# Sums over two channel blocks in a state-space layer's output stage, made by GpSimd instead of TensorE

## The chip, the cores and the metric

The kernel runs on one core of one Trainium2 chip. The metric is the device time of one execution in microseconds (us). Engines are named as in the profile: PE is TensorE, PEld its loading of weights, DVE VectorE, ACT ScalarE, POOL GpSimd, SP SyncE, which here issues the DMAs. L491 is line 491 of the kernel before; the changed file has its lines a few numbers further down.

## The reference, cut to what matters

Four layers are run one after the other on an image of 2 x 56 x 56 positions with 128 channels. The change concerns the end of the first layer, a selective scan in two dimensions. Its input is normalized by groups and projected to twice 256 channels, `x` and `z`. The first 256 go through a 3 x 3 convolution and four scans (by rows and by columns, each forwards and backwards), whose sum is `y`. Then:

```
mu  = jnp.mean(y, axis=-1, keepdims=True)
var = jnp.mean((y - mu) ** 2, axis=-1, keepdims=True)
y = (y - mu) / jnp.sqrt(var + EPS) * out_norm_w + out_norm_b
y = y * z
return jnp.einsum('bhwd,cd->bhwc', y, out_proj_w) + out_proj_b
```

Here `z` has already gone through silu, and the mean runs over the 256 channels of a position. The result is added to the layer's input. The second layer is another scan of the same kind with four heads one after the other; the third and fourth hold attention and other mixers.

## The kernel before, in words

Positions number L = 3136 in each of two batches; a chunk is 448 of them, so there are seven chunks a batch. In the scan layers channels lie on the 128 partitions and positions along the free axis. The 256 inner channels are two blocks of 128, `ci` 0 and 1, and `y[0]` and `y[1]` are the two halves of the buffer `pair`, each 128 x 3136 in float32.

The first layer goes: preparation of batch 0 (`before`, chunk by chunk), scans of batch 0 (`scans.run`), then in one loop over chunks the outputs of batch 0 (`after`, L671) and the preparation of batch 1 (`before`, L635), scans of batch 1, then in one loop the outputs of batch 1 and the preparation of the second layer's first head (L830). So `after` runs fourteen times, in two stretches of seven, each beside the preparation of the scans that follow.

The scans carry their own written order (`manual_schedule`). Outside of them a planner places each engine's instructions by its own estimates, so the order on an engine is not the order of the source, and a change of one function can move its neighbours. Each engine then works through its list in order.

One chunk of `after`: SP loads the kept normalized input (`hout`) and the layer's input `xr`; POOL adds a bias to `xr` (L679); PE projects `hout` to the gate, one product for each block (`pz`, L683), and ACT applies silu (L687). Then `gated_tokens`: PE multiplies both blocks of `y` by a matrix whose entries are all 1/256 (`avg`) and accumulates the two, so that `pm` holds the mean of the 256 channels on every partition (L491). DVE subtracts it from each block (`yc`, L495), ACT squares (`sq0`, `sq1`, L497), POOL multiplies `yc` by the gate (L499). For each of four groups of TP = 112 positions PE makes three sums over both blocks (L509): the variance `pv` (the squares against a column of `avg`), `p1` (the gated `yc` against the output weights) and `p2` (the gate against the bias term's weights); the result has positions on partitions. ACT takes the root (L511), DVE the reciprocal (L512), and DVE scales `p1`, adds `xr` and `p2` and writes the result to `X` (L691 to L693).

Beside it in the first stretch is the convolution of batch 1: nine products on PE (L460) or nine steps on DVE (L464, L466), silu on ACT (L467), and a copy into the transposed order on POOL (L468). In the second stretch it is the second layer's normalization (L78 to L86; L83 takes the root on ACT, L86 is on POOL), scaling of copies on POOL (L848, L849), transposes (L852), projection (L855, L867) and convolution. The pieces that begin a scan (`first`, L230) lie in the same stretches.

Of buffers, the pool `one` has a single one for each name: `sq0`, `sq1`, `xr`, `t`. The PSUM pool `pp` of `pm`, `pv`, `p1`, `p2`, `pz` has one each too. Tiles from `sp` (`yc0`, `yc1`, `z0`, `z1`, `rs`, `hout`) have two. ACT must load another table when it goes from silu to the root, the exponential or softplus; these appear as loads of their own.

Of the kernel before, what the change touches and what calls it, by code (L numbers as in the profile page):

```python
# [14 lines left out]
F32 = mybir.dt.float32  # L15
BF16 = mybir.dt.bfloat16
AF = mybir.ActivationFunctionType
ALU = mybir.AluOpType
# [7 lines left out]
TP = 112  # L26
NT = L // TP
CH = 448
# [449 lines left out]
    nc.gpsimd.memset(pad[:, :, PAD - 1 : PAD], 0.0)  # L478


def gated_tokens(k, pools, nch, y, gate, avg, mean, w1, w2, c, nb):

    nc = k.nc
    sp, pp, one = pools
    cs = slice(CH * c, CH * (c + 1))
    pm = pp.tile([128, CH], F32, name="pm")
    for ci in range(nch):  # L490
        nc.tensor.matmul(pm, lhsT=avg, rhs=y[ci][:, cs], start=ci == 0, stop=ci == nch - 1)  # L491
    sq, yz = [], []
    for ci in range(nch):
        yc = sp.tile([128, CH], F32, name=f"yc{ci}")
        nc.vector.tensor_tensor(yc, y[ci][:, cs], pm, ALU.subtract)  # L495
        s = one.tile([128, CH], F32, name=f"sq{ci}")
        nc.scalar.activation(s, yc, AF.Square)  # L497
        sq.append(s)
        nc.gpsimd.tensor_tensor(yc, yc, gate[ci], ALU.mult)  # L499
        yz.append(yc)  # L500
    n = w1[0].shape[-1]
    pv = pp.tile([TP, 4 * nb], F32, name="pv")
    p1 = pp.tile([TP, 4, n], F32, name="p1")
    p2 = pp.tile([TP, 4, n], F32, name="p2")
    for i in range(4):
        ts = slice(TP * i, TP * (i + 1))
        for out, m, rhs in ((pv[:, nb * i : nb * (i + 1)], sq, [mean] * nch), (p1[:, i], yz, w1), (p2[:, i], gate, w2)):
            for ci in range(nch):
                nc.tensor.matmul(out, lhsT=m[ci][:, ts], rhs=rhs[ci], start=ci == 0, stop=ci == nch - 1)  # L509
    rs = sp.tile([TP, 4 * nb], F32, name="rs")  # L510
    nc.scalar.activation(rs, pv, AF.Sqrt, bias=k.eps[:TP])  # L511
    nc.vector.reciprocal(rs, rs)  # L512
    return p1, p2, rs
# [45 lines left out]
def layer0(k, d, big, follow):  # L559


    nc, tc, X = k.nc, k.tc, k.X
    with ExitStack() as ctx:
# [13 lines left out]
        avg = wp.tile([128, 128], F32, name="avg0")  # L577
# [3 lines left out]
        y, row, col = ([t[:, 0:L] for t in big[i : i + 2]] for i in (0, 2, 4))  # L581
# [28 lines left out]
        with ExitStack() as sctx:  # L610
# [47 lines left out]
            def outputs(ip):  # L658

                ow = load(nc, ip, d["L0_out_w"], "out_w")  # L660
                outs = []
                for n in ("onw", "onb"):
                    t = ip.tile([128, 2, C], F32, name="outonw") if n == "onw" else ow
                    for ci in range(2):
                        nc.vector.tensor_scalar(t[:, ci], ow[:, ci], W[n][:, ci : ci + 1], None, ALU.mult)
                    outs.append([t[:, ci] for ci in range(2)])
                bias = ip.tile([TP, C], F32, name="out_b0")
                nc.sync.dma_start(bias, d["L0_out_b"][0].partition_broadcast(TP))
                return outs, bias

            def after(b, pools, c, outs, bias):  # L671


                sp, pp, one = pools
                h = sp.tile([128, CH], F32, name="hout")
                nc.sync.dma_start(h, kept[b, :, CH * c : CH * (c + 1)])
                xr = one.tile([TP, 4, C], F32, name="xr")
                nc.sync.dma_start(xr, d["x"][b, CH * c : CH * (c + 1)].rearrange("(j p) c -> p j c", p=TP))
                nc.gpsimd.tensor_tensor(xr, xr, bias.unsqueeze(1).to_broadcast([TP, 4, C]), ALU.add)  # L679
                gate = []  # L680
                for ci in range(2):
                    ps = pp.tile([128, CH], F32, name="pz")
                    nc.tensor.matmul(  # L683
                        ps, lhsT=W["in_w"][:, 256 + 128 * ci : 384 + 128 * ci], rhs=h, start=True, stop=True
                    )
                    z = sp.tile([128, CH], F32, name=f"z{ci}")
                    nc.scalar.activation(z, ps, AF.Silu, bias=W["in_b"][:, 2 + ci : 3 + ci])  # L687
                    gate.append(z)
                p1, p2, rs = gated_tokens(k, pools, 2, y, gate, avg, avg[:, 0:1], outs[0], outs[1], c, 1)
                t = one.tile([TP, 4, C], F32, name="t")  # L690
                nc.vector.tensor_tensor(t, p1, rs.unsqueeze(2).to_broadcast([TP, 4, C]), ALU.mult)  # L691
                nc.vector.tensor_tensor(xr, xr, p2, ALU.add)
                nc.vector.tensor_tensor(  # L693
                    X[:, 4 * c : 4 * (c + 1), b, :].rearrange("p j (c g) -> p j g c", g=4),
                    t.rearrange("p j (g c) -> p j g c", g=4), xr.rearrange("p j (g c) -> p j g c", g=4), ALU.add,
                )

            for b in range(B):
                with ExitStack() as bctx:
                    sp = bctx.enter_context(k.pool(f"mid{b}", 2))  # L700
                    pp = bctx.enter_context(k.pool(f"pmid{b}", psum=True))
                    cp = bctx.enter_context(k.pool(f"pcon{b}", 2, psum=True))
                    ip = bctx.enter_context(k.pool(f"pads{b}"))
                    if b > 0:
                        outs = outputs(ip)
# [17 lines left out]
                    for c in range(NCH + 1):  # L723
                        if b == 0 and c == 2:
                            norm(1, (ap, tp), groups)
                        if b > 0 and c < NCH:
                            after(b - 1, (sp, pp, ip), c, *outs)
                        before(b, (sp, cp), c, pads, diag)
                        if c == 2:
                            scans.first(cp)  # L730
                scans.run()
        with ExitStack() as bctx:
            sp = bctx.enter_context(k.pool("midl", 2))
            pp = bctx.enter_context(k.pool("pmidl", psum=True))
            ip = bctx.enter_context(k.pool("onel"))
            outs = outputs(ip)
            chunk = follow(bctx)
            for c in range(NCH + 1):
                if c < NCH:
                    after(B - 1, (sp, pp, ip), c, *outs)  # L740
                chunk(c)
# [1302 lines left out]
```

## Time and profile before

| | |
|---|---|
| median of 3 runs | 9105.64 us (9102.32 to 9109.07) |
| the profiled execution, its own time | 9098.37 us |
| its span | 9096.6 us |
| PE busy | 7993.2 us (88%) |
| DVE busy | 7088.0 us (78%) |
| POOL busy | 6350.1 us (70%) |
| ACT busy | 3854.8 us (42%) |
| mean granted PE clock | 0.951 |

The span is the time from the first to the last recorded instruction of one execution, which was taken by the hardware profiler; that execution's own time is a little more. The busy shares are averages over stages with different limits: what an edit is worth is read in its own stage. A matrix product in float32 leaves two records on PE here, so that the 28 products into `pm` are counted as 56.

### The profile page before, as it was taken

The page shows a single profiled execution, that of the slowest core. Times are in us where ns is not written, and L with a number is a line of the kernel's source. Part 1 is how long each engine was busy: PE and PEld are TensorE (multiplying, and loading weights), DVE is VectorE, ACT ScalarE, POOL GpSimd, SP SyncE. Part 2 cuts the span into 40 slices and gives each one's busy share as a digit, 9 for nine tenths or more (in the row PEclk, how much of TensorE's full clock was granted, in tenths as well). Part 3 has the DMA queues.
Part 4 walks back from the last instruction along what each step waited for, and adds up shares of the span by engine and source line. Part 5 has one row for each costly group of instructions (what it writes and reads, how often), then busy time and mean ns, then how long its engine had stood idle before and what let it go on. Part 6 is the DMA issues. An engine that isn't in the chain of part 4 may idle for free. (4 is left out here: it accounts for less than half of the span.)

```text
span 9096.6 us, 93496 instructions
## 1 busy us (share of the span) xinstructions
PE 7993.2 (88%) x28687; PEld 4765.5 (52%) x28687; DVE 7088.0 (78%) x7568; ACT 3854.8 (42%) x6644; POOL 6350.1 (70%) x4066
## 2 busy tenths in 40 slices
PE   8888888888887888888888888699999999999998
PEld 4444445444444444444444444355688888874555
DVE  8999998999997997998999899511467667665442
ACT  4555545555555555554554555433211111114331
POOL 6999996999996997998899799566311111115551
PEclk9999999999999998998999899799999999999999
DMA  5666664666664995996898699100233333320004
GB/s 159 221 221 220 222 212 127 221 221 220 222 220 110 230 226 134 227 228 157 203 227 204 157 227 224 39 3 3 85 96 105 104 94 110 93 63 8 14 1 135
DMA packets 780368, 1362.92 MB, mean 150 GB/s; under 512 B 133101, under 2 KB 405486, under 8 KB 779834
## 3 DMA queue, kind: packets, MB, share of 16 engines
q1 hardware_dynamic: 779866, 1356.95, 53.1%
q8 instruction: 227, 3.72, 0.2%
q14 instruction: 275, 2.25, 0.1%
HBM read 1317.03 MB, written 39.60 MB: 149 GB/s over the span
## 5 line engine op out<-in xcount | busy, mean ns | idle before, releaser
L430 POOL TENSOR_TENSOR p<-h,c 128x784 f32<-128x784 f32 x2048 | 3761.2, 1864 | 115.0 <-DVE h L358 33.1
L358 DVE TENSOR_TENSOR_SCAN h<-a,state,h 128x784 f32<-128x784 f32 x1536 | 2791.8, 1840 | 51.6 <-ACT a L339 28.7
L378 PE MATMUL acc<-p,center 128*128 128x392 f32 x4096 | 1499.0, 499 | 22.7 <-POOL p L430 20.8
L378 PE MATMUL acc<-p,ident 128*128 128x392 f32 x4096 | 1491.9, 498 | 6.7 <-POOL p L430 6.7
L417 DVE TENSOR_TENSOR h<-du,b 128x784 f32<-128x784 f32 x1408 | 1336.7, 949 | 75.6 <-PE b L364 70.4
L339 ACT ACTIVATE a<-delta,L0A 128x784 f32<-128x784 f32 x1024 | 939.3, 918 | 973.4 <-DVE h L358 971.5
L339 ACT ACTIVATE a<-delta,L1A 128x784 f32<-128x784 f32 x1024 | 939.2, 917 | 908.3 <-DVE h L358 905.3
L364 PE MATMUL b<-three,sel 96*128 96x512 bf16 (+1 forms) x2816 | 728.6, 341 | 563.9 <-DVE h L417 460.1
L433 POOL TENSOR_TENSOR h<-du,b 128x784 f32<-128x784 f32 x640 | 1190.3, 1860 | 4.1 <-PE pcv L460 4.1
L378 PEld LDWEIGHTS acc<-p,center 128*128 128x128 f32 x4096 | 740.9, 192 | 536.8 <-POOL p L430 60.2
L378 PEld LDWEIGHTS acc<-p,ident 128*128 128x128 f32 x4096 | 743.9, 192 | 512.8 <-POOL p L430 26.5
L1089 POOL TENSOR_TENSOR total<-total,e 128x448 f32<-128x448 f32 (+1 forms) x644 | 735.6, 1142 | 326.0 <-ACT e L1078 286.0
L358 DVE TENSOR_TENSOR_SCAN h<-a,h 128x784 f32<-128x784 f32 x512 | 901.7, 1780 | 36.7 <-ACT a L339 21.1
L364 PEld LDWEIGHTS <-sel 96*128 96x128 bf16 x2816 | 281.5, 100 | 1230.9 <-issue 1048.6
L1572 DVE TENSOR_TENSOR u<-u,cv 128x512 f32<-128x512 f32 x1024 | 623.7, 681 | 326.6 <-PE cv L1559 325.4
L1603 POOL TENSOR_TENSOR u<-u,S 128x1024 f32<-128x1024 f32 x64 | 150.0, 2365 | 1041.0 <-DVE S L1572 1041.0
L1078 ACT ACTIVATE e<-sc 128x448 f32<-128x448 f32 (+1 forms) x700 | 377.2, 543 | 723.0 <-PE sc L1076 596.3
L1574 ACT COPY u<-cv 128x512 f32<-128x512 f32 x256 | 149.5, 587 | 829.3 <-PE cv L1559 775.7
L1673 PE MATMUL pj<-u,Wm 128*128 128x196 f32 (+8 forms) x1536 | 354.7, 384 | 5.7 <-DVE A L1679 5.7
L1076 PE MATMUL sc<-big 128*128 128x448 f32 (+1 forms) x700 | 323.4, 547 | 15.4 <-ACT e L1078 12.3
L1070 PE MATMUL av<-e,big 128*128 128x448 f32 (+1 forms) x700 | 320.9, 545 | 1.2 <-DVE e L1083 1.0
L1653 POOL TENSOR_TENSOR both<-mpm 128x512 f32<-128x512 f32 x32 | 40.6, 1269 | 392.3 <-DVE Wm L1709 272.8
(452 smaller groups left out, 11251.1 us busy)
## 6 DMA issues: line engine op xcount, KB each, us to landing
c<-rows SPq DMA_DIRECT2D x1024, 392.0 KB, 4.0
c<-rows SPq DMA_DIRECT2D x2048, 196.0 KB, 4.8
b<-rows SPq DMA_DIRECT2D x320, 392.0 KB, 4.5
b<-rows SPq DMA_DIRECT2D x640, 196.0 KB, 4.6
H<-raw SPq DMA_DIRECT2D x32, 1568.0 KB, 7.6
wC<-win SPq DMA_DIRECT2D x64, 576.0 KB, 6.4
w<-in_L_weight_dram SPq DMA_DIRECT2D x52, 512.0 KB, 6.3
wA<-win SPq DMA_DIRECT2D x64, 384.0 KB, 5.6
```

Of the source, the lines that this page charges most:

```text
L339: self.k.nc.scalar.activation(x["a"], g["delta"][ci], AF.Exp, scale=self.w["A"](g["kd"], ci, x["n"]))
L358: self.k.nc.vector.tensor_tensor_scan(h, a, h, start, ALU.mult, ALU.add)
L364: self.k.nc.tensor.matmul(ps[:, c0:c1], lhsT=self.w["selB"](x["n"]), rhs=x["g"]["three"][:, c0:c1], start=True, stop=True)
L378: nc.tensor.matmul(job["acc"][:, i, 0:392], lhsT=self.w["sum"], rhs=x["p"][:, 392 * i : 392 * (i + 1)], start=False, stop=n == NS - 1,)
L417: nc.vector.tensor_tensor(one["h"], one["g"]["du"][one["ci"]], one["b"], ALU.mult)
L430: nc.gpsimd.tensor_tensor(now["p"], now["h"], now["c"], ALU.mult)
L433: nc.gpsimd.tensor_tensor(three["h"], three["g"]["du"][three["ci"]], three["b"], ALU.mult)
L1076: nc.tensor.matmul(ps[:n], lhsT=keys[b][:, KT * j : KT * j + n], rhs=q, start=True, stop=True)
L1078: nc.scalar.activation(e[:n], ps[:n], AF.Exp, scale=scale)
L1089: nc.gpsimd.tensor_tensor(total[:n], total[:n], e[:n], ALU.add)
L1572: nc.vector.tensor_tensor(place(o), place(o), ps, ALU.add)
L1673: nc.tensor.matmul(ps[:, lo - c0 : hi - c0], lhsT=Ws[f][:, eo, r, :], rhs=u[:, b, f, lo - a0 : hi - a0], start=f == 0, stop=f == 1,)
```

## The change

In `gated_tokens` POOL adds the two blocks of `y` first, into a tile `both`, and PE multiplies that one tile by `avg`. After both squares are made, POOL adds the second to the first, and PE makes each of the four pieces of `pv` from that sum in one product. `both` has the name `sq1` and so uses the buffer of the second square. The products that remain are also written in another order: all of `p2`, all of `p1`, then `pv`. Three parameters that had only one value in use go.

```diff
-def gated_tokens(k, pools, nch, y, gate, avg, mean, w1, w2, c, nb):
+def gated_tokens(k, pools, y, gate, avg, w1, w2, c):
...
+    both = one.tile([128, CH], F32, name="sq1")
+    nc.gpsimd.tensor_tensor(both, y[0][:, cs], y[1][:, cs], ALU.add)
     pm = pp.tile([128, CH], F32, name="pm")
-    for ci in range(nch):
-        nc.tensor.matmul(pm, lhsT=avg, rhs=y[ci][:, cs], start=ci == 0, stop=ci == nch - 1)
+    nc.tensor.matmul(pm, lhsT=avg, rhs=both, start=True, stop=True)
...
         nc.gpsimd.tensor_tensor(yc, yc, gate[ci], ALU.mult)
         yz.append(yc)
+    nc.gpsimd.tensor_tensor(sq[0], sq[0], sq[1], ALU.add)
     n = w1[0].shape[-1]
-    pv = pp.tile([TP, 4 * nb], F32, name="pv")
+    pv = pp.tile([TP, 4], F32, name="pv")
     p1 = pp.tile([TP, 4, n], F32, name="p1")
     p2 = pp.tile([TP, 4, n], F32, name="p2")
-    for i in range(4):
-        ts = slice(TP * i, TP * (i + 1))
-        for out, m, rhs in ((pv[:, nb * i : nb * (i + 1)], sq, [mean] * nch), (p1[:, i], yz, w1), (p2[:, i], gate, w2)):
-            for ci in range(nch):
-                nc.tensor.matmul(out, lhsT=m[ci][:, ts], rhs=rhs[ci], start=ci == 0, stop=ci == nch - 1)
+    tiles = [slice(TP * i, TP * (i + 1)) for i in range(4)]
+    for p, m, w in ((p2, gate, w2), (p1, yz, w1)):
+        for i, ts in enumerate(tiles):
+            for ci in range(2):
+                nc.tensor.matmul(p[:, i], lhsT=m[ci][:, ts], rhs=w[ci], start=ci == 0, stop=ci == 1)
+    for i, ts in enumerate(tiles):
+        nc.tensor.matmul(pv[:, i : i + 1], lhsT=sq[0][:, ts], rhs=avg[:, 0:1], start=True, stop=True)
...
-                p1, p2, rs = gated_tokens(k, pools, 2, y, gate, avg, avg[:, 0:1], outs[0], outs[1], c, 1)
+                p1, p2, rs = gated_tokens(k, pools, y, gate, avg, outs[0], outs[1], c)
```

More of the change, by code (lines that the diff above doesn't have):

```diff
@@ L500, in gated_tokens @@
         yz.append(yc)
+    nc.gpsimd.tensor_tensor(sq[0], sq[0], sq[1], ALU.add)
     n = w1[0].shape[-1]
-    pv = pp.tile([TP, 4 * nb], F32, name="pv")
+    pv = pp.tile([TP, 4], F32, name="pv")
     p1 = pp.tile([TP, 4, n], F32, name="p1")
     p2 = pp.tile([TP, 4, n], F32, name="p2")
-    for i in range(4):
-        ts = slice(TP * i, TP * (i + 1))
-        for out, m, rhs in ((pv[:, nb * i : nb * (i + 1)], sq, [mean] * nch), (p1[:, i], yz, w1), (p2[:, i], gate, w2)):
-            for ci in range(nch):
-                nc.tensor.matmul(out, lhsT=m[ci][:, ts], rhs=rhs[ci], start=ci == 0, stop=ci == nch - 1)
-    rs = sp.tile([TP, 4 * nb], F32, name="rs")
+    tiles = [slice(TP * i, TP * (i + 1)) for i in range(4)]
+    for p, m, w in ((p2, gate, w2), (p1, yz, w1)):
+        for i, ts in enumerate(tiles):
+            for ci in range(2):
+                nc.tensor.matmul(p[:, i], lhsT=m[ci][:, ts], rhs=w[ci], start=ci == 0, stop=ci == 1)
+    for i, ts in enumerate(tiles):
+        nc.tensor.matmul(pv[:, i : i + 1], lhsT=sq[0][:, ts], rhs=avg[:, 0:1], start=True, stop=True)
+    rs = sp.tile([TP, 4], F32, name="rs")
     nc.scalar.activation(rs, pv, AF.Sqrt, bias=k.eps[:TP])
```

## The prediction

> **What bounds the kernel now.** I read the page for the whole, then, for the two stretches in which the changed function runs, busy times, groups of instructions and the time line. The chain that ended last covers only the program's final instructions and says nothing here.
>
> The products into the tile `pm` (count, least/median/most ns, first to last start):
>
> ```profile
> L491 PE MATMUL pm<-pair,avg x56: 539/539/643, 1364.3 to 2826.9; 128*128 128x448 f32 x56
> ```
>
> The busy times of the two stretches and of the second one's tail (start:end, length, busy us of PE, PEld, DVE, ACT, POOL, then the granted PE clock, DMA share, GB/s):
>
> ```profile
> 1362.70:1490.90 128.20, 116.00 (x534) 75.55 (x534) 92.85 (x140) 68.26 (x97) 53.62 (x47) 0.97 0.18 50
> 2750.00:2885.00 135.00, 106.10 (x514) 67.80 (x513) 85.17 (x159) 82.74 (x119) 61.96 (x66) 0.90 0.14 34
> 2845.00:2885.00 40.00, 25.04 (x74) 13.22 (x73) 21.11 (x36) 23.98 (x30) 13.66 (x11) 0.71 0.06 15
> ```
>
> Only 263 us of 9097 are touched: seven chunks between batch 0's scans and batch 1's (first stretch), seven between batch 1's scans and the second layer's (second). The scans on either side have a written order and take none of it. In the first stretch PE is busy for 116 of 128 us: it sets the pace, with short waits. In the second it is busy for 106 of 135, but only 25 of the last 40, where a chain through all engines decides.
>
> The time line of PE through a chunk, then DVE's and POOL's at the same place (start, length, operation, number of records; what it waited for in brackets):
>
> ```profile
> 1397.02 1.64 PE L509 MATMUL pv<-avg,sq 128*112 128x1 f32 x16
> 1398.53 1.00 PE L646 MATMUL pcv<-hin,L0in_w 128*128 128x448 f32 x2
> ...
> 1402.34 0.47 PE L509 MATMUL p<-outonw,yc 128*112 128x128 f32 x2 [2.07 <-POOL yc L499]
> ...
> 1403.62 1.67 PE L491 MATMUL pm<-pair,avg 128*128 128x448 f32 x4
> 1405.13 0.60 PE L509 MATMUL p<-out_w,z 128*112 128x128 f32 x4
> ```
>
> ```profile
> 1391.91 6.74 POOL L468 COPY big<-big 128x448 f32<-128x448 f32 x1 [4.96 <-ACT big L467]
> ...
> 1412.80 6.58 DVE L466 SCALAR_TENSOR_TENSOR cv<-pad,L0taps,cv 128x448 f32<-128x448 f32 x5
> ```
>
> A product leaves two records. Eight `pv` products hold PE from 1397.02 to 1398.53, so 0.19 us each; two `pm` products from 1403.62 to 1405.13, so 0.75 us each. PE waits in between for `yc`, which POOL makes. And POOL and DVE block one another: a copy that takes 0.99 us alone took 6.74 while DVE ran its convolution, and five steps of that convolution took 6.58 instead of 5 x 0.68 = 3.4 while POOL was at work.
>
> **What the Trainium skill says.** "SBUF — State Buffer", Who interferes with whom: a DVE instruction with two SBUF inputs and a GpSimd instruction that reads SBUF exclude each other for the whole instruction, whichever begins first. The convolution step (`pad`, `cv`) has two such inputs, `yc`'s subtraction has one and a PSUM bank; the two lines above agree, and `yc` L495 keeps 606 to 622 ns throughout. "ScalarE: Activation LUTs", What ACT_TABLE_LOAD costs: about 1283 ns, and a drain of about 1380; the trace has loads of 1283 ns, and the drain isn't seen: L511's load at 1371.82 is followed by its activation at 1373.12. "TensorE: Matmul & The Clock Gate", What's actually happening: an idle TensorE falls to half rate; the tail's mean clock is 0.71, and eighteen records of the last convolution took 8.48 us there against 6.93 elsewhere.
>
> **The change, part by part.** All sums are against the profiled execution (9098.37 us, span 9096.6); the median of the runs shown is 7.3 us above it, and I shift by that at the end.
>
> *Products removed.* One `pm` product and four `pv` products a chunk: 0.75 + 4 x 0.19 = 1.5 us of PE, 7 times in each stretch: 10.5 and 10.5 us. The other sixteen products stay. In the first stretch PE is the pace and nearly all of it should count; in the second about half, 5 us, since PE idles for 29 of 135 us and the tail has no such products.
>
> *Adds put on POOL.* Two a chunk, 28 in all, each like L499 (two SBUF inputs, 128x448): 1.13 us, so 15.8 us in each stretch. POOL is busy 53.6 of 128 and 62.0 of 135 us, so there is room. Their cover: `both` of chunk c+1 needs only `y`, and in the changed order it stands right after the add of the squares of chunk c, ahead of the `yc` products and a 7 us convolution on PE. It is late only at the first chunk: it must await ACT's last copy of `y` (ends 1366.1) and takes 1.13, where PE did the second product from 1366.15 to 1367.2; the mean comes about 1.0 us later. The add of squares stands ahead of the same chunk's `yc` products on POOL, and `pv` is asked for after the convolution, so it is ready; without that cover PE would wait up to 1.13 us a chunk. The buffer of `both` is that of the second square: it is free once POOL itself has added the squares, so no new wait across engines, but `pm` can no longer run before that add.
>
> *Blocking.* In the first stretch L466 took 58.4 us for 72 x 0.684 = 49.2, L468 22.3 for 14 x 0.99 = 13.9, L499 18.2 for 15.8, L679 10.1 for 8.9: together 21 us lost for 40 us of POOL's own work. At that rate 15.8 more cost 8 us, shared by two engines with slack. PE already waits 6.8 us for POOL's `yc`, and ACT 9.0 for DVE's convolution; I let half through, 4 us (bounds 0 and 8). In the second stretch convolutions are fewer (L466 28.2 for 27.2, L849 10.3 for 6.4, L693 9.4 for 7.5, L679 10.0 for 8.9: 8 us lost for 50): 2.5 us, all let through.
>
> *Order.* The scheduler moves other work. All `p2` products now stand before the `p1` ones, which need POOL: 7 x 0.22 us of cover for `yc`, a small gain that I leave uncounted. ACT's table loads fall from 299 to 297. What counts is the second stretch's tail. Before, between the squares of the last normalization and its root, ACT does other things:
>
> ```profile
> 2860.28 0.41 ACT L81 ACTIVATE sq<-nrm 112x256 f32<-112x256 f32 x1
> 2860.70 1.28 ACT L339 ACT_TABLE_LOAD   x1
> 2862.00 0.92 ACT L339 ACTIVATE a<-delta,L1A 128x784 f32<-128x784 f32 x1
> 2862.94 1.28 ACT L467 ACT_TABLE_LOAD   x1
> 2864.23 0.67 ACT L467 ACTIVATE big<-cv,L1conv_b 128x448 f32<-128x448 f32 x1
> 2864.92 1.28 ACT L83 ACT_TABLE_LOAD   x1
> 2866.21 0.30 ACT L83 ACTIVATE st<-st,eps 112x8 f32<-112x8 f32 x1
> ```
>
> POOL's `nrm`, PE's transposes, the projection and the last convolution all wait for that root. In the changed order only L83's load lies between: 1.28 + 0.92 + 1.28 + 0.67 = 4.2 us go. The subtraction, sum and reciprocal also stand together on DVE. Against it, seven convolution steps that came after the last L693 now stand ahead of it; DVE has idle time there, but up to 7 x 0.68 = 4.8 us could be late. I take 4 us net (bounds -1 and 6). On SP four loads and two stores change places with neighbours, with nothing queued behind them that waits: nothing, or a us if a load comes late (POOL waits 21 us for `xr`'s loads, and PE not at all for that).
>
> *Sum.* First stretch: -10.5 + 1.0 + 4 = -5.5. Second: -5 + 2.5 - 4 = -6.5. Together **-12 us**: span 9085, own time 9086, median 9105.6 - 12 = **9093.6 us**.
>
> **The rivals.** *PE's time comes through whole.* Speaks for it: PE's busy share in the first stretch. Against: its waits for POOL. -10.5 + 1 - 10.5 - 5.5 = -25.5: 9080 us, faster.
>
> *POOL and DVE take PE's place.* Their excluding work in the first stretch is 72 x 0.61 (the step's pitch in a run of four at 1405.87) + 9 x 0.45 + 7 x 1.07 + 2 x 0.97 = 57 on DVE and 40 on POOL, 97 of 128 us; with the adds it is 113, where PE has 105 left. Against: they overlap a little, and seven chunks leave them different gaps. The first stretch then gives nothing and the second 2: 9104 us, no change.
>
> *POOL's queue sets the pace (the other side).* If the two adds lie ahead of a waited-for POOL result in every chunk, 2.26 us x 14 = 32 are paid and only PE's part that isn't waiting, about 11, comes back: +21, 9127 us. It decides once more than about two thirds of the adds stand on the path (21 of PE's removal against 32). Against: PE waits for `yc` seven times in the first stretch (6.8 us) and five in the second (2.5 us), of fourteen `yc` in each, and POOL idles for over half of both. That the change doesn't cut the products at all is excluded: the built order has 14 `pm` and 56 `pv` products instead of 28 and 112.
>
> **How the numbers follow.** My forecast 0.45, PE's time whole 0.20, POOL and DVE in its place 0.25, POOL's queue 0.10. A measurement of this kernel can tell about 0.2%, 18 us, from no change. Faster by more than that: nearly all of the second case and the forecast's edge, 0.22; slower: the last case and a little, 0.12; within: 0.66. The forecast's own range is 9087 to 9101 (blocking 0 or 8, tail 6 or -1); to leave out no more than two in ten I go from 9078, past the second case, to 9116, halfway to the last.
>
> **What would show it.** Right: PE's busy time in each stretch down by about 10 us; 28 new POOL adds near 1.13 us, some at twice that; the first scan of batch 1, at 1490.9 before, near 1485; that of the second layer, at 2883.7, near 2872; nothing else longer. Wrong, towards slow: PE's waits for POOL's `yc` well above 6.8 us, `pv` waiting for the new add, L466 above 62 us in the first stretch. Wrong, towards fast: those waits unchanged, with both starts some 10 us earlier each. It would also fail if the scans themselves, 96% of the time, ran differently.

## The result, and the profile after

The changed kernel is slower: median 9117.6 us against 9102.25 us (17 runs of each), ratio 1.0022, interval 1.0015 to 1.0028 (the medians alone give 1.0017). The forecast was 9093.6 us, with a range up to 9116. The profiled execution of the changed kernel took 9120.5 us, span 9118.7, which is 22.1 us over the profiled span before.

Everything below is read from the lengths of the two stretches. A length runs from the end of the last product into `acc` (the scans of a batch are over) to the start of the first scan instruction on DVE (batch 1's scans begin, or the second layer's).

| | first stretch | second stretch | sum |
|---|---|---|---|
| before | 1364.44 to 1490.92: 126.5 us | 2753.95 to 2883.74: 129.8 us | 256.3 us |
| after | 1361.82 to 1490.52: 128.7 us | 2751.02 to 2905.37: 154.4 us | 283.1 us |

A length comes from one execution and can be some us off: the first stretch began anywhere from 1358.7 to 1366.4 us in the kernels below, though nothing ahead of it was changed. The whole runs tell how far off. Outside the two stretches the traces of the nineteen other kernels hold 8837 us on average; what a kernel's median leaves beside that is an estimate of its two lengths together, and those measured lie within 4.4 us of it. The exception is the kernel before: its 256.3 us lie some 9 us below (the execution profiled took 9098.4 us, its medians here 9101 to 9107). Where a difference is taken from that kernel, the ratios of whole runs are therefore the better guide, and I read little into a difference below 6 us from one pair of traces.

The busy times of the two stretches of the kernel after (start:end, length, busy us of PE, PEld, DVE, ACT, POOL, granted PE clock, DMA share, GB/s):

```profile
1362.70:1490.50 127.80, 106.96 (x460) 67.02 (x460) 102.64 (x131) 67.12 (x97) 76.51 (x53) 0.95 0.17 48
2751.10:2905.40 154.30, 110.02 (x430) 67.86 (x428) 91.15 (x157) 80.91 (x117) 75.87 (x70) 0.78 0.11 28
```

The second stretch of the kernel before, from its own start to its own end:

```profile
2754.00:2883.70 129.70, 101.43 (x500) 65.36 (x498) 79.86 (x156) 82.73 (x119) 57.30 (x56) 0.89 0.13 32
```

In the first stretch PE has 74 records fewer than in the window shown before, which makes 9 us less of busy time, and the stretch is no shorter. In the second it has 70 fewer and is busy *longer*, 110 us against 101, at a clock of 0.78 where it was 0.89. POOL gained 23 us in the first and 19 in the second.

What PE waited for in the second stretch (us in total, times, longest), and its time line in the middle of it:

```profile
PE pt L857 <- POOL nrm L86: 14.0, 4, 9.8
PE p L512 <- POOL yc L501: 11.5, 6, 3.3
PE pv L514 <- POOL sq L503: 6.7, 3, 3.1
PE pz L688 <- ACT z L692: 3.6, 2, 3.4
...
PE pm L493 <- POOL sq L491: 2.7, 1, 2.7
```

```profile
2825.10 1.13 PE L688 MATMUL pz<-hout,L0in_w 128*128 128x448 f32 x2 [3.41 <-ACT z L692]
2826.02 0.64 PE L512 MATMUL p<-out_w,z 128*112 128x128 f32 x2
2829.30 0.77 PE L512 MATMUL p<-outonw,yc 128*112 128x128 f32 x2 [2.65 <-POOL yc L501]
2832.12 1.66 PE L514 MATMUL pv<-avg,sq 128*112 128x1 f32 x8 [2.05 <-POOL sq L503]
2833.64 1.84 PE L493 MATMUL pm<-sq,avg 128*128 128x448 f32 x2
...
2844.28 0.92 PE L688 MATMUL pz<-hout,L0in_w 128*128 128x448 f32 x2
2845.04 0.85 PE L514 MATMUL pv<-avg,sq 128*112 128x1 f32 x8
```

Three waits end within 8 us, two of them for POOL, and until about 2842 nearly every product takes twice its time: `pm` 1.84 us for its two records instead of 0.92, eight `pv` records 1.66 instead of 0.85. The first of the three is for ACT, at a time when POOL itself stood idle (for 9.4 us, up to 2825.7), so not all of this place is POOL's doing. Before, PE waited in the second stretch 16.4 us for `nrm`, 2.5 for `yc` and 1.8 for a square from ACT.

The same happens at the first chunk of the first stretch. After, then before:

```profile
1364.73 1.66 PE L493 MATMUL pm<-sq,avg 128*128 128x448 f32 x2 [2.90 <-POOL sq L491]
1366.18 1.70 PE L688 MATMUL pz<-hout,L0in_w 128*128 128x448 f32 x2
1367.67 1.28 PE L651 MATMUL pcv<-hin,L0in_w 128*128 128x448 f32 x2
1371.30 1.23 PE L514 MATMUL pv<-avg,sq 128*112 128x1 f32 x8 [2.35 <-POOL sq L503]
```

```profile
1364.29 0.92 PE L491 MATMUL pm<-pair,avg 128*128 128x448 f32 x2
1366.15 1.02 PE L491 MATMUL pm<-pair,avg 128*128 128x448 f32 x2 [0.95 <-ACT pair L398]
1368.49 0.36 PE L509 MATMUL pv<-avg,sq 128*112 128x1 f32 x2 [1.32 <-ACT sq L497]
1368.71 1.00 PE L683 MATMUL pz<-hout,L0in_w 128*128 128x448 f32 x2
```

Waits of 2.90 and 2.35 us in place of 0.95 (the first block's product had run ahead of that one) and 1.32, and two spells of PE at half rate between 1365 and 1375, where it had none before.

### The profile page after: what moved, and what is told of

Its sections match the earlier page's. It is cut to its first block, busy times and chain, and to the rows that moved or that the text cites. A ratio compares the mean times of both kernels' runs of the same rounds, so it can differ in the third digit from the quotient of the medians.

```text
span 9118.7 us, 93256 instructions
## 1 busy us (share of the span) xinstructions
PE 7999.0 (88%) x28547; PEld 4763.3 (52%) x28547; DVE 7106.0 (78%) x7568; ACT 3853.3 (42%) x6642; POOL 6385.9 (70%) x4094
```

## The experiments

Theories. *Load*: POOL's time counts, whoever waits for the adds. *Chain*: what counts is that the mean and the variance now wait for POOL. *Order*: what counts is that `pv` now stands behind `p1`, or that the scheduler reshuffled the rest. *Blocking*: what counts is that POOL's reads and DVE exclude each other. The lengths are those of one execution each; ratios are of whole runs, to the kernel before, measured beside it, with 95% intervals.

| kernel | first | second | ratio |
|---|---|---|---|
| before | 126.5 | 129.8 | 1 |
| after | 128.7 | 154.4 | 1.0022 (1.0015 to 1.0028) |
| order_only | 120.7 | 133.4 | 0.9989 (0.9980 to 0.9997) |
| half_no_adds | 114.2 | 143.1 | 0.9990 (0.9982 to 0.9999) |
| adds_full_products | 132.0 | 154.0 | 1.0024 (1.0013 to 1.0034) |
| adds_old_order | 134.5 | 153.5 | 1.0026 (1.0015 to 1.0036) |
| half_no_adds_old_order | 120.8 | 146.7 | 1.0001 (0.9993 to 1.0009) |
| adds_unused | 136.3 | 147.5 | 1.0025 (1.0017 to 1.0034) |
| memsets_unused | 131.8 | 147.3 | 1.0016 (1.0009 to 1.0022) |
| adds_of_16 | 120.3 | 144.0 | 0.9994 (0.9986 to 1.0002) |
| both_in_hout | 137.2 | 144.4 | 1.0021 (1.0013 to 1.0029) |
| both_add_only | 142.4 | 143.2 | 1.0023 (1.0014 to 1.0032) |
| squares_add_only | 123.9 | 140.7 | 1.0006 (0.9998 to 1.0014) |
| adds_dve | 129.1 | 132.2 | 0.9994 (0.9985 to 1.0002) |
| p2_pv_p1 | 122.9 | 141.0 | 0.9993 (0.9985 to 1.0001) |
| adds_dve_p2_pv_p1 | 127.1 | 139.8 | 0.9998 (0.9990 to 1.0006) |
| gating_dve | 117.4 | 133.7 | 0.9983 (0.9976 to 0.9989) |
| gating_half_dve | 116.7 | 139.2 | 0.9993 (0.9986 to 0.9999) |
| before_gating_dve | 114.4 | 137.4 | 0.9985 (0.9978 to 0.9992) |
| change_gating_dve | 126.8 | 140.8 | 0.9999 (0.9991 to 1.0007) |

### The change taken apart: order, halved products, adds

`order_only`, against the changed kernel (the adds out, the products doubled again):

```
-    both = one.tile([128, CH], F32, name="sq1")
-    nc.gpsimd.tensor_tensor(both, y[0][:, cs], y[1][:, cs], ALU.add)
-    nc.tensor.matmul(pm, lhsT=avg, rhs=both, start=True, stop=True)
+    for ci in range(2):
+        nc.tensor.matmul(pm, lhsT=avg, rhs=y[ci][:, cs], start=ci == 0, stop=ci == 1)
...
-    nc.gpsimd.tensor_tensor(sq[0], sq[0], sq[1], ALU.add)
...
+        for ci in range(2):
-        nc.tensor.matmul(pv[:, i : i + 1], lhsT=sq[0][:, ts], rhs=avg[:, 0:1], start=True, stop=True)
+            nc.tensor.matmul(pv[:, i : i + 1], lhsT=sq[ci][:, ts], rhs=avg[:, 0:1], start=ci == 0, stop=ci == 1)
```

> The kernel before with the changed order of products alone: per chunk all p2, then all p1, then all pv (two products each, as before), no adds on GpSimd, two pm products. Theory 'adds' (GpSimd's adds lie on the path and make the loss): the first scan of batch 1 starts near 1491 and that of the second layer within 5 us of 2884 (before: 1490.9 and 2883.7), ratio 1.000. Theory 'order' (pv behind p1, so the root and X come late): the second layer's first scan near 2900, as with the whole change (2905.4), ratio 1.0015 or more.

`half_no_adds`, against the changed kernel:

```
-    nc.gpsimd.tensor_tensor(both, y[0][:, cs], y[1][:, cs], ALU.add)
-    nc.tensor.matmul(pm, lhsT=avg, rhs=both, start=True, stop=True)
+    nc.tensor.matmul(pm, lhsT=avg, rhs=y[1][:, cs], start=True, stop=True)
...
-    nc.gpsimd.tensor_tensor(sq[0], sq[0], sq[1], ALU.add)
...
-        nc.tensor.matmul(pv[:, i : i + 1], lhsT=sq[0][:, ts], rhs=avg[:, 0:1], start=True, stop=True)
+        nc.tensor.matmul(pv[:, i : i + 1], lhsT=sq[1][:, ts], rhs=avg[:, 0:1], start=True, stop=True)
```

> The changed order and the halved products without either add: pm averages the second block of y alone and pv the second block of squares alone, so one half of the mean and of the variance is left out. It shows what the removed products are worth by themselves. Theory 'adds': first scan of batch 1 near 1481 (10.5 us of PE less), that of the second layer near 2868 (5 more), ratio 0.998. Theory 'GpSimd and VectorE set the pace of the first stretch anyway': first scan of batch 1 at 1487 or later. Theory 'order': second layer's near 2890, whatever the first stretch does.

`adds_full_products`, against the changed kernel:

```
+    for _ in range(2):
-    nc.tensor.matmul(pm, lhsT=avg, rhs=both, start=True, stop=True)
+        nc.tensor.matmul(pm, lhsT=avg, rhs=both, start=True, stop=True)
...
+        for _ in range(2):
-        nc.tensor.matmul(pv[:, i : i + 1], lhsT=sq[0][:, ts], rhs=avg[:, 0:1], start=True, stop=True)
+            nc.tensor.matmul(pv[:, i : i + 1], lhsT=sq[0][:, ts], rhs=avg[:, 0:1], start=True, stop=True)
```

> The whole change with every pm and pv product issued twice (the second overwrites the first), so TensorE has as many products as before and GpSimd has its adds: the adds alone. Theory 'TensorE's saving is swallowed by blocking in the first stretch': first scan of batch 1 near 1500 (after plus 10.5), second layer's near 2920. Theory 'GpSimd sets the pace, TensorE has slack': first scan of batch 1 at 1494 or less, second layer's within 6 us of 2905 plus what the first stretch moved.

`adds_old_order` is the changed kernel, and `half_no_adds_old_order` is `half_no_adds`, with the products in the old nesting (the latter with `sq[1:]` for `sq`):

```
-    for p, m, w in ((p2, gate, w2), (p1, yz, w1)):
-        for i, ts in enumerate(tiles):
...
     for i, ts in enumerate(tiles):
...
+        for p, m, w in ((pv[:, i : i + 1], sq, [avg[:, 0:1]] * 1), (p1[:, i], yz, w1), (p2[:, i], gate, w2)):
+            for ci in range(len(w)):
+                nc.tensor.matmul(p, lhsT=m[ci][:, ts], rhs=w[ci], start=ci == 0, stop=ci == len(w) - 1)
```

> The whole change, but with pv, p1, p2 issued tile by tile as before. Theory 'adds': still slow, first scan of the second layer near 2900 to 2910, and PE waits for GpSimd's add of squares in most chunks; ratio 1.002. Theory 'order': the second layer's first scan back at 2885 or earlier, ratio 1.000 or below.

> Half of the pm and pv products, no adds (one block of y and one of squares left out of the mean and the variance), products tile by tile in the order of the kernel before. With the kernel before and the changed kernel in the old order it splits the old order's loss in two. Theory 'adds': the removed products alone gain, first scan of batch 1 near 1487 (3.5 less than 1490.9) and that of the second layer between 2875 and 2885. Theory 'a reshuffled order is worth 10 us either way in the second stretch': that one anywhere from 2870 to 2895.

What each part is worth, wherever two of these kernels are written to differ in it alone (us; the planner's order on the engines differs too in each pair). The last column is an estimate from the ratios, good to about 10 us:

| part | first stretch | second stretch | whole runs |
|---|---|---|---|
| changed order of products | -5.8, -6.7, -5.8 | +3.6, -3.6, +0.9 | -10, -10, -4 |
| half of the products | -5.6, -6.5, -3.3 | +16.9, +9.7, +0.4 | +1, +1, -2 |
| two adds on POOL | +13.7, +14.5, +11.3 | +6.8, +11.3, +20.6 | +23, +29, +32 |

In the first stretch the three pairs of each part agree: the adds eat all that the order and the halved products save there. In the second the order does nothing to be read, the adds cost 7 to 21 us, and the halved products save *nothing* in any of three pairs. Of the +16.9 some 9 may be the short lengths of the kernel before; the +9.7 doesn't rest on it. How the second stretch's 25 us divide between adds and halving depends on which is done first. Over the whole program the halved products are worth nothing that can be read, and the adds cost 23 to 32 us in all three pairs. *Order* falls as the cause of the loss: alone it is the faster kernel.

### Load or chain

`adds_unused`, against `order_only` (`h` is the gate input, dead after `pz`; the second add stands after the gating):

```
+    nc.gpsimd.tensor_tensor(h, y[0][:, cs], y[1][:, cs], ALU.add)
     pm = pp.tile([128, CH], F32, name="pm")
...
+    nc.gpsimd.tensor_tensor(h, y[0][:, cs], y[1][:, cs], ALU.add)
     n = w1[0].shape[-1]
```

> The run with the changed order alone, plus two GpSimd adds a chunk of the same size at the places of the changed kernel's, each of the two blocks of y and written over the dead gate input, so that nothing waits for them; pm and pv take two products as before. On every other engine the order of instructions is nearly that of the changed order alone. Theory 'load' (GpSimd's time and its exclusion of VectorE make the loss, whoever waits): first scan of batch 1 near 1494, that of the second layer near 2900. Theory 'chain' (the adds cost because the mean and the variance wait for them): first scans within 3 us of 1484 and within 5 of 2879.

`memsets_unused`, against `adds_unused`, at both places:

```
-    nc.gpsimd.tensor_tensor(h, y[0][:, cs], y[1][:, cs], ALU.add)
+    nc.gpsimd.memset(h, 0.0)
+    nc.gpsimd.memset(h, 0.0)
```

> The run with the unused adds again, with two memsets of 128x448 in the place of each add (some 0.5 us each, so GpSimd's queue holds nearly the same time), written over the same dead input. A memset reads no SBUF. Order on PE, DVE and ACT as in the run with the changed order alone. Theory 'queue' (what counts is the time that GpSimd's in-order queue is held): first scan of batch 1 near 1498, that of the second layer near 2905, as with the unused adds (1500.8 and 2910.8). Theory 'exclusion' (what counts is that a reading GpSimd and VectorE block each other): first scans within 4 us of 1484.0 and 2878.5.

`adds_of_16`, against `half_no_adds`:

```
+    few = slice(CH * c, CH * c + 16)
+    nc.gpsimd.tensor_tensor(y[1][:, few], y[0][:, few], y[1][:, few], ALU.add)
     pm = pp.tile([128, CH], F32, name="pm")
...
+    nc.gpsimd.tensor_tensor(sq[1][:, :16], sq[0][:, :16], sq[1][:, :16], ALU.add)
```

> The run with half the products and no adds, plus the two GpSimd adds a chunk on 16 of the 448 columns only, in place (15/16 and more of one block's part is left out of the mean and the variance). So pm and pv wait for GpSimd as in the change, while GpSimd loses only some 0.1 us an add; the order on the other engines is that of half the products without adds (1480.6 and 2885.5). Theory 'load': first scans within 3 us of these. Theory 'chain' (waiting for GpSimd's turn costs, however short the add): near the changed kernel's 1490.5 and 2905.4.

These are the cleanest pairs: between `memsets_unused` and `order_only` the instructions of PE and ACT stand in the same order throughout, those of DVE but for one place, and between `adds_of_16` and `half_no_adds` those of PE, DVE, ACT and SP.

Adds that no other engine's work waits for cost 15.6 and 14.1 us. They take 8.9 + 8.7 = 17.6 us of POOL's time in the first stretch and 8.6 + 8.3 = 16.9 in the second, so 0.89 and 0.84 of it come through, from an engine that is idle for half of both. Memsets, which read nothing that DVE could be kept from, take 13.3 us of POOL's time in each stretch (28 of 0.47) and cost 11.2 and 13.9. The ratios say the same of whole runs: 33 us for the adds and 25 for the memsets, by estimate. So *load* holds and *blocking* isn't needed for it: the convolution step L466 takes 60.6 us in the first stretch of `adds_unused`, against 59.6 in `order_only`.

Adds of 16 columns, with which `pm` and `pv` wait for POOL as in the change, cost 0.9 us in the second stretch (on POOL they take 0.2 to 0.4 us each, not the 0.1 that I had expected): no *chain* there. They add in place, though, so the buffer that the change shares between the blocks' sum and the second square isn't in this test. In the first stretch they cost 6.2. (The first scan's start, by which I had meant to judge, hides that: 1480.10 against 1480.58, but the stretch began 6.7 us earlier.) Its place is mostly the first chunk. `adds_of_16`, then `half_no_adds`:

```profile
1361.77 1.23 PE L493 MATMUL pm<-pair,avg 128*128 128x448 f32 x2 [2.00 <-POOL pair L491]
1363.84 1.86 PE L688 MATMUL pz<-hout,L0in_w 128*128 128x448 f32 x2 [0.84 <-DMA hout<-kept]
```

```profile
1368.13 1.02 PE L491 MATMUL pm<-pair,avg 128*128 128x448 f32 x2 [1.70 <-ACT pair L398]
1370.29 1.02 PE L685 MATMUL pz<-hout,L0in_w 128*128 128x448 f32 x2 [1.15 <-DMA hout<-kept]
```

Both wait 2.8 us in all; only the first then ran at half rate, to about 1372. Over the stretch PE is busy 6.0 us longer and idle 0.2 us longer. So the 6.2 us are the clock's, and that waiting for the adds made them isn't shown.

How POOL's time reaches the end. POOL, then PE, of `order_only` around the gating of one chunk:

```profile
1459.93 1.13 POOL L500 TENSOR_TENSOR yc<-yc,z 128x448 f32<-128x448 f32 x1 [0.54 <-ACT sq L498]
1461.02 1.42 POOL L683 TENSOR_TENSOR xr<-xr,out_b 112x512 f32<-112x512 f32 x1
1462.39 1.44 POOL L468 COPY big<-big 128x448 f32<-128x448 f32 x1
1463.80 1.12 POOL L500 TENSOR_TENSOR yc<-yc,z 128x448 f32<-128x448 f32 x1
```

```profile
1464.97 1.78 PE L510 MATMUL p<-outonw,yc 128*112 128x128 f32 x14 [2.06 <-POOL yc L500]
1466.59 1.64 PE L513 MATMUL pv<-avg,sq 128*112 128x1 f32 x16
```

The same place in `memsets_unused`:

```profile
1467.91 0.47 POOL L490 MEMSET hout<- 128x448 f32 x1 [0.80 <-PE pz L691]
1468.35 1.28 POOL L502 TENSOR_TENSOR yc<-yc,z 128x448 f32<-128x448 f32 x1
1469.56 0.47 POOL L491 MEMSET hout<- 128x448 f32 x1
1469.99 1.26 POOL L687 TENSOR_TENSOR xr<-xr,out_b 112x512 f32<-112x512 f32 x1
1471.20 0.99 POOL L468 COPY big<-big 128x448 f32<-128x448 f32 x1
1472.16 1.51 POOL L502 TENSOR_TENSOR yc<-yc,z 128x448 f32<-128x448 f32 x1
```

```profile
1473.72 2.85 PE L514 MATMUL p<-outonw,yc 128*112 128x128 f32 x14 [3.08 <-POOL yc L502]
1476.37 3.01 PE L517 MATMUL pv<-avg,sq 128*112 128x1 f32 x16
```

The two gatings of a chunk have other work between them in POOL's queue, the queue runs without a gap here, and PE stands at the end of it. One memset ahead of the first gating, one behind it and slower gatings make PE's wait 3.08 us where it was 2.06, and after it the clock halves: the fourteen records (seven products) that follow take 2.85 us instead of 1.78, the sixteen `pv` records 3.01 instead of 1.64. Over the second stretch, `order_only` and then `memsets_unused`:

```profile
2745.20:2878.50 133.30, 103.23 (x500) 66.53 (x499) 85.88 (x156) 80.03 (x117) 56.75 (x56) 0.88 0.13 32
```

```profile
2761.40:2908.70 147.30, 115.78 (x501) 75.31 (x499) 85.46 (x157) 80.26 (x117) 67.83 (x84) 0.80 0.12 29
```

PE has the same work and is busy 12.6 us longer, at a clock of 0.80 instead of 0.88; its idle time grows by only 1.4 us, and the stretch by 14.0. Here late results of POOL are paid mostly in products at half rate. It isn't always so. `adds_unused`, then `p2_pv_p1` (below), in the same stretch:

```profile
2763.30:2910.80 147.50, 108.91 (x500) 70.44 (x499) 93.32 (x157) 80.06 (x117) 73.17 (x70) 0.86 0.12 29
```

```profile
2746.60:2887.60 141.00, 114.17 (x500) 74.95 (x499) 84.10 (x157) 79.95 (x117) 58.87 (x56) 0.81 0.12 31
```

With the unused adds the 14 us are 5.7 of busy time and 8.5 of waiting. In `p2_pv_p1`, which adds nothing to POOL, PE waits 3.2 us less than in `order_only` and is busy 10.9 longer. So the clock can move the second stretch by as much with the order of the products alone, and what part of the loss goes through it isn't shown: nothing was run that holds the clock up while POOL is late.

### Where the adds are put

`both_in_hout`, against the changed kernel, with `both` now the gate input `h`:

```
-    both = one.tile([128, CH], F32, name="sq1")
     nc.gpsimd.tensor_tensor(both, y[0][:, cs], y[1][:, cs], ALU.add)
```

> The whole change, but the added blocks are written over the chunk's gate input (double-buffered, dead after the two pz products) and not into the buffer of the second square. So the next chunk's add, and with it its pm, need no longer wait for this chunk's add of squares. Theory 'coupling' (the shared buffer chains one chunk's mean to the last chunk's variance): the second layer's first scan comes 10 us or more earlier than 2905, near 2892, and the ratio falls to 1.001 or less. Theory 'blocking' (the adds keep VectorE and GpSimd off each other's work, wherever they write): first scan of batch 1 stays near 1490, that of the second layer within 6 us of 2905.

`both_add_only` takes from it the add of squares (and has two `pv` products again); `squares_add_only` is the changed kernel without `both` (and with two `pm` products).

> Changed order of products, the blocks of y added by GpSimd (written over the gate input, as in the run before) for one pm product; the squares not added, pv with two products. Against the run with the changed order alone (first scans at 1484.0 and 2878.5): theory 'each add costs alike', half of the whole: first scan of batch 1 near 1487, that of the second layer near 2892. Theory 'the mean's add is the dear one, since everything in the chunk waits for it': second layer's near 2900. Theory 'the squares' add is the dear one': near 2880.

> Changed order of products, two pm products as before; the squares added by GpSimd, one pv product each. Counterpart of the run before: theory 'each add costs alike' first scans near 1487 and 2892; theory 'the squares' add is the dear one' second layer's near 2900, with PE waiting for it ahead of pv; theory 'the mean's add is the dear one' near 2880.

Freed from the square's buffer, the second stretch is 10 us shorter (144.4), as *coupling* had it; but the add now waits for `pz`, and the first stretch is 8.5 us longer (PE waited 8.9 us there for the added blocks and 4.2 for the first load of `hout`). The ratio doesn't move. Each add alone, with its halved products, costs: the squares' 3.2 and 7.3 us over `order_only`, the blocks' 21.8 and 9.9, part of which is the wait for `pz`; by the ratios 15 and 31, an estimate. So neither is harmless; "half each" doesn't hold.

`adds_dve` has both adds on VectorE:

```
-    nc.gpsimd.tensor_tensor(both, y[0][:, cs], y[1][:, cs], ALU.add)
+    nc.vector.tensor_tensor(both, y[0][:, cs], y[1][:, cs], ALU.add)
...
-    nc.gpsimd.tensor_tensor(sq[0], sq[0], sq[1], ALU.add)
+    nc.vector.tensor_tensor(sq[0], sq[0], sq[1], ALU.add)
```

> The whole change with both adds on VectorE instead of GpSimd. Theory 'blocking by GpSimd': VectorE pays some 0.6 us an add (8.5 us a stretch) in engines with slack, and the saving of TensorE comes through: first scan of batch 1 at 1484 or earlier, that of the second layer at 2880 or earlier, ratio 0.998. Theory 'any add ahead of the mean and of the variance lengthens the chunk's chain': first scan of batch 1 near 1488, that of the second layer above 2895.

First stretch as with POOL (129.1), second 22 us shorter (132.2). The loss is gone (0.9994), but no gain is left over `order_only`. The halved products can't be cashed in by moving the adds.

`p2_pv_p1` is `order_only` with the `pv` products moved ahead of the `p1` products, and `adds_dve_p2_pv_p1` is `adds_dve` with the same move. In `p2_pv_p1` the products then read, each under its own loop over `tiles` and `ci`:

```
            nc.tensor.matmul(p2[:, i], lhsT=gate[ci][:, ts], rhs=w2[ci], start=ci == 0, stop=ci == 1)
...
            nc.tensor.matmul(pv[:, i : i + 1], lhsT=sq[ci][:, ts], rhs=avg[:, 0:1], start=ci == 0, stop=ci == 1)
...
            nc.tensor.matmul(p1[:, i], lhsT=yz[ci][:, ts], rhs=w1[ci], start=ci == 0, stop=ci == 1)
```

> No adds and no halved products: the order of products alone, p2 first, then pv, then p1, so that the root is asked for ahead of the products that wait for GpSimd's gating. If an early root matters: first scan of the second layer earlier than with p2, p1, pv (2878.5), and a ratio of 0.998. If not: within 5 us of it, ratio 0.999; a difference of 10 us in either direction would be what reshuffling the planned order is worth by itself.

> The whole change with both adds on VectorE and the products in the order p2, pv, p1. A candidate: if TensorE's saving can be had at all, here. Theory 'GpSimd is the wrong engine': ratio 0.998, first scans near 1485 and 2876. Theory 'any add lengthens the chunk's chain': no better than the order alone, ratio 0.999 to 1.000.

No gain: an early root doesn't matter. What these two do show is what a reshuffled order is worth: the second stretch is 7.6 us longer in both pairs, with the same work on every engine.

### Taking load off POOL

`gating_dve` is `order_only`, `before_gating_dve` the kernel before, and `change_gating_dve` the changed kernel, each with this one edit; `gating_half_dve` is `order_only` with it for the first block alone:

```
-        nc.gpsimd.tensor_tensor(yc, yc, gate[ci], ALU.mult)
+        nc.vector.tensor_tensor(yc, yc, gate[ci], ALU.mult)
```

> The mirror: changed order of products, no adds, all products, and the two gating multiplications a chunk moved from GpSimd to VectorE, so GpSimd loses as much work (28 of 1.13 us) as the change gave it. Theory 'load' (a us of GpSimd is a us of the end): faster, first scan of batch 1 near 1472 to 1478, second layer's near 2860, ratio 0.9975. Theory 'VectorE and GpSimd only share the time': within 4 us of 1484 and 2878, ratio 0.999.

> As the run before with only the first block's gating on VectorE and the second's left on GpSimd: half of the move. Theory 'load': half of its gain, ratio 0.998 to 0.9985. Theory 'share': ratio 0.999. If it beats both it is the better balance.

> The whole change, with the two gating multiplications a chunk on VectorE: GpSimd's load is that of the kernel before (the adds in the place of the gating), TensorE's is the changed one. Theory 'load on GpSimd' : the loss is gone, first scans near 1482 and 2880, ratio 0.999. Theory 'the adds themselves, wherever the load': still near 1490 and 2905, ratio 1.002.

> The kernel before with one edit, the two gating multiplications a chunk on VectorE; products in the old order, all of them, no adds. If GpSimd's place in the chunk's chain is what sets both stretches: faster by 10 us or more, ratio 0.9985, as with the changed order of products (0.9983). If that gain was the changed order's alone: ratio 0.9995 or above.

Two of these beat both kernels clearly: 0.9983 (0.9976 to 0.9989, median 9087.4 us) with the changed order of products, 0.9985 (0.9978 to 0.9992) with no other edit; the intervals don't tell the two apart. In the first stretch taking 14 gatings off POOL saves 12.1 us in the old order and 3.3 in the new one, which is too little to be read; in the second it saves nothing (+7.6, against the short length of the kernel before, and +0.3). The mirror works in part, then: POOL's extra time costs in both stretches, its relief pays in the first, and clearly only in the old order. Moving one of the two gatings is no better than none (0.9993).

With POOL's load back to what it was, the change's loss is gone: 0.9999 instead of 1.0022, the second stretch 13.5 us shorter. But beside `gating_dve` the adds and the halved products still cost 9.4 and 7.1 us.

## Why the prediction was wrong

- *Products removed.* The count was right: 1.5 us of PE a chunk. "Nearly all of it should count" in the first stretch held for 5.6 to 6.5 of 10.5 us, 3.3 with the adds in place; "about half, 5 us" in the second held for nothing (+0.4 to +16.9), so this step failed too. In the second stretch of `half_no_adds` 430 records keep PE busy for 100.1 us, where 500 took 103.2 in `order_only`: most of the removed time is lost again at a clock of 0.84 instead of 0.88, and PE's idle time grew from 30 to 43 us:

```profile
2742.40:2885.50 143.10, 100.13 (x431) 64.06 (x429) 86.33 (x157) 86.95 (x122) 55.98 (x56) 0.84 0.12 30
```

- *Adds put on POOL.* This step failed, and it made the sign. "POOL is busy 53.6 of 128 and 62.0 of 135 us, so there is room" inferred cover from a share of busy time. Measured: 11.3 to 14.5 us in the first stretch against 1.0 + 4, and 6.8 to 20.6 in the second against 2.5; over whole runs 23 to 32 against 7.5. The cover was argued for the adds' own results; what they delayed was everything queued behind them, above all `yc`, for which PE already waited.
- *First chunk.* The wait was right: the mean came 1.8 us later after the scans' last product than before, 1.1 of it the wait, as forecast, and 0.7 the product at half rate. That half rate, which went on behind it, was missing from the sum.
- *Blocking.* It occurred: the convolution step L466 took 70.5 us in the first stretch for 58.4 before. "SBUF — State Buffer", Who interferes with whom, of the Trainium skill describes it (a DVE instruction with two SBUF inputs contends with a GpSimd instruction that reads SBUF), and the longer steps agree. But the memsets show that the loss doesn't need it, and unused adds of the same size left L466 at 60.6 us. The term was too small and named the wrong means.
- *Order.* The gain that was left uncounted, of `p2` ahead of `p1`, is the larger part of what the change saves: 5.8 to 6.7 us in the first stretch, in all three pairs. That it is `p2`'s cover for `yc`, and not another place that the planner moved, isn't shown.
- *The tail.* As forecast, in one trace each: from the last X on DVE (2880.33) to the first scan it takes 25.0 us, from 2855.82 it took 27.9. Only L83's load is left between the squares and the root:

```profile
2884.94 0.42 ACT L81 ACTIVATE sq<-nrm 112x256 f32<-112x256 f32 x1 [2.55 <-DVE nrm L80]
2885.89 1.28 ACT L83 ACT_TABLE_LOAD   x1 [0.53 <-DVE st L82]
2887.18 0.30 ACT L83 ACTIVATE st<-st,eps 112x8 f32<-112x8 f32 x1
```

  A saving of 2.9 us against 4 forecast, too small to be read by itself; but the last X came 129.3 us into the stretch instead of 101.9.
- *The rivals.* "POOL's queue sets the pace" at +21 us was the case that came, at a chance of 0.10. Its cost of the adds held, with 0.84 to 0.89 of the time of unused adds coming through. That its sum fits as well is luck in part: it gives back 11 us for PE's products, and what came back was the order's gain. What spoke against it, five waits of 2.5 us in all and an idle POOL, was weak evidence. "POOL and DVE take PE's place" gave the first stretch's number, no gain, but not for its reason: without the adds the halved products did save there. In "PE's time comes through whole" the sum has a term of 5.5 us that isn't explained; the tail was put at 4, at most 6.
- *The signs named.* All three of the slow side came: waits for `yc` of 12.7 us instead of 6.8 in the first stretch, `pv` waiting for the add of squares (6.7 us in the second), L466 above 62 us.

What stays open: why halving the products without adds lengthened the second stretch, by 10 us where the kernel before isn't in the pair. A reshuffled order alone moved it by 7.6, so the order that came with it may be the cause; it was not held fixed while products were removed. Open too is how much the buffer shared by the blocks' sum and the second square adds there.

## What to carry to other kernels

A busy share doesn't show room: an engine idle for half of a stretch can still stand in each chunk's path, and here 0.84 to 1.04 of the time put into its queue was paid. Look at who already waits for it, and what stands ahead of those results, before giving it work; in the old order the opposite move paid. To learn what added work costs, add it with its results unused, so that the other engines keep their order. And where TensorE waits for some 2 to 3 us in every chunk, cost a further microsecond of delay at its clock too.

## What the runs showed of the hardware that I had not expected

The length of a single wait doesn't tell whether PE's clock falls. Three waits that stood alone, in the changed kernel, `adds_old_order` and `p2_pv_p1`:

```profile
1389.80 1.78 PE L512 MATMUL p<-outonw,yc 128*112 128x128 f32 x14 [2.69 <-POOL yc L501]
```

```profile
1456.65 0.47 PE L512 MATMUL p<-outonw,yc 128*112 128x128 f32 x2 [3.42 <-POOL yc L501]
1456.96 0.38 PE L512 MATMUL p<-out_w,z 128*112 128x128 f32 x2
1457.18 0.92 PE L649 MATMUL pcv<-hin,L0in_w 128*128 128x448 f32 x2
```

```profile
1400.93 0.58 PE L515 MATMUL p<-outonw,yc 128*112 128x128 f32 x2 [1.93 <-POOL yc L500]
1401.31 1.70 PE L652 MATMUL pcv<-hin,L0in_w 128*128 128x448 f32 x2
```

After 2.69 and 3.42 us PE goes on at full rate (0.92 us for two records of `pcv`), after 1.93 at half rate (1.70). And in `memsets_unused` two waits of 1.01 and 0.76 us with one short product between them were enough:

```profile
1438.62 0.47 PE L514 MATMUL p<-outonw,yc 128*112 128x128 f32 x2 [1.01 <-POOL yc L502]
1439.85 3.11 PE L514 MATMUL p<-outonw,yc 128*112 128x128 f32 x14 [0.76 <-POOL yc L502]
1442.75 1.82 PE L517 MATMUL pv<-avg,sq 128*112 128x1 f32 x14
```

What does tell is in the record of the granted clock. In all twenty traces it changes only on a grid of 3.41 us that has its own start in each execution. Over the two stretches of the twenty, a slot of that grid at full clock in which PE was busy for less than 1.4 us was followed by one at half clock in 111 of 111 cases; with 1.7 us or more, in 28 of 1127. So a wait counts by what it leaves of PE's work in a slot: several short ones add up, and one of 3 us can fall across two slots and cost nothing. That fits the two first chunks above, with 2.8 us of waiting each and only one of them at half rate.

The Trainium skill ("TensorE: Matmul & The Clock Gate", What's actually happening) tells of a free-running window of 3413 ns and a fall to half rate after an idle window. The traces agree on the window; for the fall it need not be idle here, only busy for less than about 1.4 us.
